# One copy and two squarings change places in ScalarE's order, in a graph attention kernel

## The chip, the cores and the metric

The kernel runs on one core of one Trainium2 chip. The metric is the device time of one execution in microseconds (us), as the median of several runs. In a profile, PE is TensorE (matmuls), PEld its weight loads, DVE is VectorE, ACT is ScalarE, POOL is GpSimd and SP is SyncE, which here issues nearly all the DMAs. L586 is line 586 of the kernel. PSUM is the memory that matmuls write; the kernel hands it out in pieces of 128 x 512 (banks, as its code calls them) and in pairs of two such pieces.

## The reference, cut to what matters

Sixteen images x[b] of 1024 nodes with 256 channels pass through two layers that share one 1024 x 1024 matrix adj. Everything is float32.

```python
# layer 0
fea  = x.transpose(0, 2, 1)                       # 256 x 1024 of an image
c    = mean(fea, axis=1)                          # one mean per node
A    = abs(abs(sigmoid(c_n - c_m) - 0.5) - 0.5) * 2
g    = relu((fea @ (adj * A)) * para)             # the "query graph": queries by channel
k, v = split(x @ kv_w)                            # 4 heads of 64
x1   = layernorm(x + softmax(q k^T * scale) v)    # over the channels
# layer 1
h    = relu(x1 @ w1_loop + adj @ (x1 @ w1_neigh) + b1)
h    = relu(h  @ w2_loop + adj @ (h  @ w2_neigh) + b2)
out  = layernorm(x1 + (x1 + h) * 0.5)
```

Two places matter here. One is the product of fea with the weighted matrix (the queries). The other is the layernorm of the attention's sum: it subtracts the mean, squares what is left, sums the squares over the channels and scales.

## The kernel before, in words

The program is one long list of instructions written out by hand, image by image (`run()`, L972 on); no scheduler moves anything. Each engine takes its own instructions in the order in which the Python code issues them, and a semaphore wait holds back an instruction whose data or buffer isn't ready.

For image b the loop first runs four attention units (`Attention`: scores, exponentials, denominators, outputs). Between the units it does the second layer of earlier images and prepares the weighted matrix of image b + 1. After the units, for 14 of the images, come these steps, which stand in the branch `elif more` (L1151 on):

- Steps 0 to 3 of the queries of image b + 1 (`FastQueries.step`, L560 to L577). The product is made by Strassen's method in the form with seven products, which are summed over four steps k. At each step seven matmuls run, each of 128 x 512, which the profile shows as two passes ("x2"). The sums stand in PSUM: products 1 and 6 in the two halves (banks) of one buffer, 2 and 7 in a second, 5 and 3 in a third, and 4 in a bank of its own. In step 3 the order is 1, 6, 2, 7, 4, 5, 3. The right factors come from VectorE (`times_adj`, `right`, `pair`, L494 to L496 and L542 to L558); product 6 takes the one that L551 makes.
- Beside step 1 the last attention results of image b are added up (`att.add`). Beside step 2, after its first four products, `norm.mean()` (L306 to L311) lets VectorE make the mean and subtract it from the two tiles of x, and `norm.squares()` (L313 to L316) lets ScalarE square the two tiles.
- `q.load_para()` and `kv.load()` issue three DMA loads on SP's queue.
- `FastQueries.end` (L579 to L596) puts the seven products together into the queries qT. ScalarE copies product 1 from PSUM to a tile P1 (L586); VectorE then makes the additions L587 to L590, the sums of the squares (`norm.sum_squares`, handed in as `between`, L318 to L322: two reductions L321 and one small addition), and the additions L592 to L594.
- `kv.run` (L409 on) makes keys and values of image b + 1 by the same method, first the key product 1 (L402), whose PSUM buffer is the one in which products 1 and 6 stood before. Three such buffers exist (`bufs=3`), and two single banks.
- In the middle of `kv.run`, `norm.variance` makes the reciprocal deviation (a small matmul L252, L326 on VectorE, a power on GpSimd, L328) and `q.scale` multiplies the queries by para (L600, L601).

Tiles of 128 x 1024 in SBUF (the squares, P1, U, para, kv_sums, adj and many others) come from one pool of 25 buffers (`row_tile`) that are handed out in the order of the code. A new owner waits until the last reader of the old one is done.

Of the kernel before, what the change touches and what calls it, by code (L numbers as in the profile page):

```python
# [18 lines left out]
def kernel(  # L19
# [79 lines left out]
    def row_tile(name):  # L99
        return work.tile([P, N], F32, tag="row", name=name, bufs=ROWS)  # L100
# [85 lines left out]
    def store(n, rows):  # L186
        for h in range(2):
            nc.sync.dma_start(out=far_adj[n][h], in_=rows[h])
# [275 lines left out]
    class Queries:  # L464
# [42 lines left out]
        def end(self):  # L507
            qT = work.tile([P, NC, N], F32, tag="qT", name=f"qT_{self.b}")
            for cb in range(NC):
                nc.vector.tensor_mul(qT[:, cb, :], self.pg[cb], self.para[cb])  # L510
                nc.scalar.activation(qT[:, cb, :], qT[:, cb, :], AF.Relu, scale=QSCALE)
            return qT

    class FastQueries(Queries):
# [61 lines left out]
                x_n, w_n = terms[n]  # L576
                nc.tensor.matmul(self.p[n], x_n[:, k, :], w_n, start=(k == 0), stop=(k == TJ - 1))  # L577

        def end(self, between):  # L579
            qT = work.tile([P, NC, N], F32, tag="qT", name=f"qT_{self.b}")  # L580
            u = row_tile(f"U_{self.b}")
            h0, h1 = ts(0, FB), ts(1, FB)
            p = self.p
            add = nc.vector.tensor_add
            p1 = row_tile(f"P1_{self.b}")[:, h0]
            nc.scalar.copy(p1, p[1])  # L586
            add(u[:, h0], p1, p[6])  # L587
            add(qT[:, 0, h0], p1, p[2])
            add(u[:, h1], u[:, h0], p[7])
            add(qT[:, 1, h0], u[:, h1], p[4])  # L590
            between()
            add(qT[:, 1, h1], u[:, h1], p[5])  # L592
            add(u[:, h0], u[:, h0], p[5])
            add(qT[:, 0, h1], u[:, h0], p[3])  # L594
            self.qT = qT
            return qT  # L596
# [375 lines left out]
    def run():  # L972
# [11 lines left out]
        q = Queries(0, x_first)  # L984
# [41 lines left out]
        qT = q.end()  # L1026
# [3 lines left out]
        for b in range(B):  # L1030
            more = b + 1 < B
            att = Attention(b, xB, qT, kT, v)
            c1, c2, c3 = (convs.get(b - k) for k in (1, 2, 3))
            both = Joined(c1, c2) if c2 else None
            if c1 and more:
                xb, blocked = coming
            if c2 and more:
                c2.load_h1()

            def load_next():  # L1040
                nonlocal coming
                if b + 2 < B:
                    coming = load_x(b + 2, str(b + 2)), load_blocked(b + 2, str(b + 2))

            def gap0():
                row = means(q, xb, str(b + 1))
                c1.inner()
                if both:
                    c2.load_x()
                    both.fetch(2, 3)  # L1050
                    both.left(nc.gpsimd)
                row()
                ready["xT"] = channel_major(blocked, f"xT_{b + 1}")

            def weigh_first():
                q.times_adj(0)
                q.times_adj(TJ)
                q.right(0)

            def gap1():  # L1060
                for t in (0, TJ):
                    q.load(t)
                if both:
                    both.fetch(1, 4)
                    both.run({1: (lambda: q.left(nc.gpsimd),),
                              2: (lambda: att.add(0, 1),),
                              6: (lambda: q.likeness(0), lambda: c3 and c3.moments()),
                              7: (lambda: q.likeness(TJ),),
                              5: (weigh_first,),
                              4: (lambda: c3 and c3.finish(out[b - 3]),),  # L1070
                              3: (c1.turn_blocks,)})
                else:
                    q.left(nc.gpsimd)
                    for t in (0, TJ):
                        q.likeness(t)
                    store("01", rows01)
                    c1.first(rows01, lambda: (att.add(1), adj_sums(rows01, 1), adj_sums(rows01, 2), weigh_first()))
                    c1.turn_blocks()

            def gap2():  # L1080
                if both:
                    c2.last()

            between = [gap0, gap1, gap2] if c1 and more else []
            if more:
                q = (FastQueries if c1 else Queries)(b + 1, xb)
            for u in range(len(UNITS)):
                att.scores(u)
                if u == 1 and between:
                    kv = KeysValues(b + 1, ready["xT"])  # L1090
                    kv.sums()
                if u == 3 and between:
                    for t in (2, TJ + 2, 3, TJ + 3):
                        q.load(t)
                    for t in (2, TJ + 2, 3, TJ + 3):
                        q.likeness(t)
                    q.right(1)
                if u and (not between or u != 2 and not both):
                    att.add(u - 1)
                att.outputs(u)  # L1100
                if u == 2 and more:
                    if c1:
                        for t in (1, TJ + 1):
                            q.load(t)
                            q.likeness(t)
                            q.times_adj(t)
                    else:
                        for t in range(3):
                            q.load(t)
                            q.weigh(t)  # L1110
                if u < 3 and between:
                    between[u]()
                if u == 0 and more and not between:
                    means(q, xb, str(b + 1))()
            norm = BlockedNorm(xB, att.sums, str(b))
            if more and not c1:
                kv = KeysValues(b + 1, ready["xT"])
                for t in range(3, NT):
                    q.load(t)
                for t in range(3, NT):  # L1120
                    q.likeness(t)
                tiles[2] = adj_blocked(2)
                q.times_adj(3)
                q.step(0)
                q.times_adj(4)
                q.step(1)
                att.add(3)
                for mt in (3, 5, 6, 7):
                    tiles[mt] = adj_blocked(mt)
                q.load_para()  # L1130
                q.times_adj(5)
                q.step(2)
                q.step(3)
                norm.mean()
                q.times_adj(6)
                q.times_adj(7)
                q.step(4)
                norm.squares()
                norm.sum_squares()
                q.step(5)  # L1140
                q.step(6)
                kv.sums()
                kv.load()
                norm.variance()
                xB = load_blocked(b + 1, f"a{b + 1}")
                q.step(7)
                qT = q.end()
                load_next()
                kT, v = kv.run(later=lambda: (norm.scale(), norm.spread(), turn_adj((2, 3))))
                turn_adj((5, 6, 7))  # L1150
            elif more:  # L1151
                q.pair(2)
                q.step(0)
                q.step(1, lambda: att.add(*((2, 3) if both else (3,))))
                q.pair(3)
                q.step(2, lambda: (norm.mean(), norm.squares()))
                q.load_para()
                kv.load()
                q.step(3)
                qT = q.end(norm.sum_squares)  # L1160
                xB = load_blocked(b + 1, f"a{b + 1}")
                load_next()
                kT, v = kv.run(norm.variance, q.scale)
                if not c2:
                    adj_sums(rows01, 3)
                norm.scale()
                norm.spread()
            else:
                c2.load_h1()
                c2.load_x()  # L1170
                both.fetch(2, 3)
                c1.inner()
                both.left(nc.gpsimd)
                both.fetch(1, 4)
                both.run({1: (lambda: att.add(3),), 2: (norm.mean, norm.squares, norm.sum_squares), 7: (norm.variance,),
                          5: (norm.scale, norm.spread)})
                c1.turn(0)
                c2.last()
                c1.turn(1)
            convs[b] = GraphConv(b, norm.x1T, norm.nodes)  # L1180
# [16 lines left out]
    with tc.manual_schedule():  # L1197
        run()
# [14 lines left out]
    with tc.If(count < P):  # L1213
        with tc.For_i(0, B, 1) as b:
            xb = load_x(b, "z")
            xT = channel_major(load_blocked(b, "z"), "xT_z")
            q = Queries("z", xb)
# [48 lines left out]
```

## Time and profile before

| quantity | value |
|---|---|
| median of 3 runs | 2163.99 us (2163.22 to 2164.79) |
| the profiled execution | 2163.48 us |
| its span, first to last instruction | 2161.6 us |
| granted TensorE clock, mean | 0.999 of full speed |
| time of one image in the middle of the run (first key product to first key product) | 133.1 us |
| squares L316 | 32 times, 1.06 us each |
| copy P1 L586 | 14 times, 0.57 us each |
| additions L587 | 14 times, 0.69 us each |
| para and kv_sums loads, issue to landing | 3.9 us and 5.7 us (medians) |
| bytes moved by DMA | 290.73 MB, 134 GB/s over the span |

The profile is of one execution. Its page gives each engine's busy time over the whole span. The list of waits sums up, for each pair "who waited for whom", the idle time of the waiting engine, with the number of waits and the longest one. The timeline lists instructions of an engine by start time; neighbours of one kind are merged into one row with their number ("x2"), and square brackets give the idle time of the engine before the row and what ended it. The ends of matmuls are modelled, so the distance between two starts says more about TensorE than a duration does. Instructions of the same kind repeat almost to the hundredth of a microsecond from image to image, so that one image can stand for the others.

### The profile page before, as it was taken

The numbers are of one execution on the slowest core, as the hardware profiler recorded it, in microseconds if no ns is written. First come the engines' busy times: TensorE is split into PE (matmuls) and PEld (weight loads), VectorE is DVE, ScalarE is ACT, GpSimd is POOL, SyncE is SP. The second block draws the span as 40 slices with busy tenths as digits, with TensorE's granted clock in tenths as the row PEclk, the third lists the DMA queues.
The fourth block names the chain that finished last, engine by engine and source line by source line (L and its number), as shares of the span: only waits on it lengthen the run. The fifth ranks groups of instructions, "written<-read, shape, count | busy, mean of one in ns | idle before, by whom it ended". The sixth has DMA issues, their size and how long they took to land.

```text
span 2161.6 us, 23756 instructions
## 1 busy us (share of the span) xinstructions
PE 2146.5 (99%) x8360; PEld 1021.1 (47%) x8360; DVE 1904.5 (88%) x2350; ACT 1041.0 (48%) x1374; POOL 362.7 (17%) x201
## 2 busy tenths in 40 slices
PE   9999999999999999999999999999999999999998
PEld 5344444444444444454544445454454444544354
DVE  5999988988999899899898998989889898998965
ACT  5745535545345454445443554445553445535412
POOL 1010120211303113030120302203021130211021
PEclk9999999999999999999999999999999999999999
DMA  9393654736558265472755627555374563733442
GB/s 236 117 146 117 148 154 110 164 97 134 148 128 182 86 132 156 130 173 88 122 167 127 160 88 120 172 127 156 88 134 159 127 156 106 140 134 90 125 137 99
DMA packets 612191, 290.73 MB, mean 134 GB/s; under 512 B 504800, under 2 KB 569696, under 8 KB 612064
## 3 DMA queue, kind: packets, MB, share of 16 engines
q1 hardware_dynamic: 611792, 288.87, 54.5%
q8 instruction: 68, 1.11, 0.2%
q14 instruction: 59, 0.48, 0.1%
q10 hardware_dynamic: 272, 0.26, 0.0%
HBM read 242.35 MB, written 46.72 MB: 134 GB/s over the span
## 4 chain that ended last, share of the span: by engine, by line


## 5 line engine op out<-in xcount | busy, mean ns | idle before, releaser
L628 ACT ACTIVATE pr<-s 128x1024 f32<-128x1024 f32 x512 | 476.1, 1054 | 175.0 <-PE s L625 174.2
L634 DVE TENSOR_TENSOR acc<-acc,pr 128x1024 f32<-128x1024 f32 x384 | 487.2, 1269 | 40.8 <-DVE acc L634 0.5
L625 PE MATMUL s<-qT,kT 64*128 64x512 f32 x2048 | 456.8, 596 | 0.0
L647 PE MATMUL av<-pr,v 128*64 128x512 f32 x2048 | 453.6, 595 | 0.0
L625 PEld LDWEIGHTS s<-qT,kT 64*128 64x128 f32 x2048 | 191.6, 186 | 236.6 <-ACT pr L628 112.5
L328 POOL TENSOR_TENSOR rstd<-rstd,neg_half 128x32 f32<-128x32 f32 x16 | 99.8, 6238 | 1125.6 <-DVE rstd L326 1125.6
L647 PEld LDWEIGHTS av<-pr,v 128*64 128x64 f32 x2048 | 141.3, 137 | 298.7 <-issue 291.6
L490 ACT ACTIVATE wg<-c_row,c_col 128x1024 f32<-128x1024 f32 x128 | 146.1, 1141 | 75.5 <-DVE accB L636 66.1
L496 DVE SCALAR_TENSOR_TENSOR wg<-wg,adj 128x1024 f32<-128x1024 f32 x128 | 150.0, 1210 | 12.3 <-ACT wg L491 12.3
L931 PE MATMUL hu_ps<-adj,R 128*128 128x512 f32 x360 | 158.0, 595 | 0.0
L491 ACT ACTIVATE wg<-wg 128x1024 f32<-128x1024 f32 x128 | 135.3, 1057 | 4.1
L316 ACT ACTIVATE sq<-xB_a 128x1024 f32<-128x1024 f32 x32 | 33.7, 1056 | 211.5 <-DVE xB_a L311 210.4
L577 PE MATMUL g_ps<-wg,S 128*128 128x512 f32 x224 | 116.4, 601 | 0.0
L577 PE MATMUL g_ps<-T,S 128*128 128x512 f32 x224 | 115.7, 598 | 0.1
L632 DVE TENSOR_TENSOR acc<-pr,pr 128x1024 f32<-128x1024 f32 x64 | 83.2, 1300 | 31.6 <-ACT pr L628 31.6
L577 PE MATMUL g_ps<-wg,x 128*128 128x512 f32 x224 | 109.0, 599 | 0.0
L931 PE MATMUL hu_ps<-adjT,t 128*128 128x512 f32 x240 | 105.7, 592 | 0.0
L931 PEld LDWEIGHTS hu_ps<-adj,R 128*128 128x128 f32 x360 | 67.3, 190 | 78.9 <-issue 78.9
L636 DVE STREAM_TRANSPOSE accB<-acc 128x1024 f32<-128x1024 f32 x64 | 79.7, 1246 | 2.2
L947 ACT COPY snap<-hu_ps 128x512 f32<-128x512 f32 x15 | 8.8, 585 | 150.3 <-PE hu_ps L931 150.3
L639 DVE TENSOR_REDUCE den_part<-accB 128x32 f32<-128x1024 f32 x64 | 78.1, 1220 | 2.2
L819 PE MATMUL h_ps<-w2n_sb,uT 128*128 128x256 f32 x240 | 72.7, 385 | 0.0
(204 smaller groups left out, 2997.2 us busy)
## 6 DMA issues: line engine op xcount, KB each, us to landing
adj<-in_adj_dram SPq DMA_DIRECT2D x128, 512.0 KB, 5.1
adj<-adjT SPq DMA_DIRECT2D x120, 512.0 KB, 10.2
para<-in_L_gnn_para_dram SPq DMA_DIRECT2D x32, 512.0 KB, 3.9
xB_a<-in_x_dram SPq DMA_DIRECT2D x128, 128.0 KB, 4.3
x1d<-xB_a SPq DMA_DIRECT2D x128, 128.0 KB, 3.5
x<-x1d SPq DMA_DIRECT2D x16, 1024.0 KB, 15.1
xB<-in_x_dram SPq DMA_DIRECT2D x120, 128.0 KB, 4.5
x<-in_x_dram SPq DMA_DIRECT2D x15, 1024.0 KB, 7.0
```

Source lines behind the costliest of these rows:

```text
L328: nc.gpsimd.tensor_tensor(self.rstd, self.rstd, neg_half, ALU.pow)
L490: nc.scalar.activation(wg, self.c_row, AF.Abs, bias=self.c_col[:, t:t + 1], scale=-1.0)
L491: nc.scalar.activation(wg, wg, AF.Tanh, scale=-0.5)
L496: nc.vector.scalar_tensor_tensor(wg, wg, 1.0, self.adj.pop(t), op0=ALU.add, op1=ALU.mult)
L577: nc.tensor.matmul(self.p[n], x_n[:, k, :], w_n, start=(k == 0), stop=(k == TJ - 1))
L625: nc.tensor.matmul(ps[:, ts(s, FB)], self.kT[rows, pair, ts(mt, P)], self.qT[rows, pair, ts(j, FB)], start=True, stop=True)
L628: nc.scalar.activation(pr, ps, AF.Exp)
L632: nc.vector.tensor_add(acc, self.pr[0], pr)
L634: nc.vector.tensor_add(acc, acc, pr)
L636: nc.vector.transpose(accB, acc)
L647: nc.tensor.matmul(pav[s * HD:(s + 1) * HD, :], self.v[:, mt, pair * P + s * HD:pair * P + (s + 1) * HD], self.pr[mt][:, ts(s, FB)], start ...
L931: nc.tensor.matmul(dst, self.x[n][:, k, :], half_adj[w][:, k, :] if w else of_rows(rows, k), start=(start and k == 0), stop=(k == TJ - 1), ...
```

## The change

The squaring of the two tiles of x is no longer issued beside step 2 but inside `FastQueries.end`, right after ScalarE's copy of product 1. In ScalarE's order the copy L586 then stands ahead of the two squares L316, in each of the 14 images that go through `FastQueries`. The row buffers of the squares are taken from the pool at that later place too, after those of para, kv_sums, U and P1. The numbers of lines below L586 move by one.

```diff
-        def end(self, between):
+        def end(self, between, aside):
             qT = work.tile([P, NC, N], F32, tag="qT", name=f"qT_{self.b}")
...
             p1 = row_tile(f"P1_{self.b}")[:, h0]
             nc.scalar.copy(p1, p[1])
+            aside()
             add(u[:, h0], p1, p[6])
...
-                q.step(2, lambda: (norm.mean(), norm.squares()))
+                q.step(2, norm.mean)
                 q.load_para()
                 kv.load()
                 q.step(3)
-                qT = q.end(norm.sum_squares)
+                qT = q.end(norm.sum_squares, norm.squares)
```

## The prediction

> **What bounds the kernel now.** I read the page's busy times first, then the list of waits, then the timeline around one hand-over between the query graph and the keys, engine by engine.
>
> ```profile
> PE 2146.5 (99%) x8360; PEld 1021.1 (47%) x8360; DVE 1904.5 (88%) x2350; ACT 1041.0 (48%) x1374; POOL 362.7 (17%) x201
> ```
>
> TensorE works nearly all the time, so only an edit that lets its matmuls start earlier can shorten the span; time saved on ScalarE (48%) or VectorE (88%) counts only where TensorE waits for it. The waits show one such chain:
>
> ```profile
> ACT sq L316 <- DVE xB_a L311: 210.4, 16, 16.2
> DVE U L587 <- ACT P L586: 23.2, 14, 1.7
> PEld k_ps L402 <- DVE U L587: 15.4, 14, 1.2
> ```
>
> Each of the 14 images whose queries go through `FastQueries` has it once: ScalarE's squares (L316) wait for the subtraction of the mean (L311), the copy P1 (L586) stands behind them, VectorE's first addition (L587) waits 1.7 us for P1, and the first key product (L402) waits for that addition, since it writes the PSUM buffer that P1 and the addition read. The idle time given is not yet what TensorE loses. For that I take its start times:
>
> ```profile
> 1043.52 1.02 PE L577 MATMUL g_ps<-wg,x 128*128 128x512 f32 x2
> 1044.53 1.13 PE L577 MATMUL g_ps<-T,S 128*128 128x512 f32 x2
> 1045.49 1.02 PE L577 MATMUL g_ps<-wg,x 128*128 128x512 f32 x2
> 1046.35 1.02 PE L577 MATMUL g_ps<-wg,S 128*128 128x512 f32 x2
> 1047.21 1.02 PE L577 MATMUL g_ps<-T,x 128*128 128x512 f32 x2
> 1048.06 1.02 PE L577 MATMUL g_ps<-T,S 128*128 128x512 f32 x2
> 1048.92 1.02 PE L577 MATMUL g_ps<-wg,S 128*128 128x512 f32 x2
> 1050.21 1.13 PE L402 MATMUL k_ps<-xT,kvw_sb 128*128 128x512 f32 x2 [0.27 <-DVE U L587]
> 1051.17 1.05 PE L406 MATMUL v_ps<-kvw_sb,xT 128*128 128x128 f32 x8
> 1052.07 1.02 PE L402 MATMUL k_ps<-xT,kvw_sb 128*128 128x512 f32 x2
> 1052.93 1.05 PE L406 MATMUL v_ps<-kvw_sb,xT 128*128 128x128 f32 x8
> ```
>
> The seven rows with g_ps are step 3, products 1, 6, 2, 7, 4, 5, 3 in that order, each in two passes. Product follows product every 0.86 us; the first key product comes 1.29 us after product 3, so it is 0.43 us late. It also takes 0.96 us until its successor starts, while the second key product takes 0.86: the second pass of a product that had to wait comes 0.10 us late too. ScalarE and VectorE in the same stretch:
>
> ```profile
> 1046.77 2.19 ACT L316 ACTIVATE sq<-xB_a 128x1024 f32<-128x1024 f32 x2 [13.63 <-DVE xB_a L311]
> 1048.87 0.57 ACT L586 COPY P<-g_ps 128x512 f32<-128x512 f32 x1
> ```
>
> ```profile
> 1045.45 2.36 DVE L311 TENSOR_TENSOR xB_a<-xB_a,mean 128x1024 f32<-128x1024 f32 x2
> 1049.47 0.69 DVE L587 TENSOR_TENSOR U<-P,g_ps 128x512 f32<-128x512 f32 x1 [1.66 <-ACT P L586]
> ```
>
> ScalarE is idle for 13.63 us and then does the copy last.
>
> **What the Trainium skill says.** "TensorE: Matmul & The Clock Gate", section "Architectural detail: the array is 16× 32×32, not 1× 128×128", has ScalarE and VectorE as strict FIFOs, while TensorE may pull a weight load ahead of matmuls in flight. The trace agrees: P1 could not pass the squares although its data were there 3 us before, and a product that waited shows its two weight loads together and a late second pass. "Perfetto Trace Analysis", section "Tensor Engine Instruction (MATMUL, LD_WEIGHTS)", says that a matmul's end is an estimate; it shows here as 1.02 us given for products that follow each other every 0.86, and is why I count starts and not the idle 0.27. "PSUM — Partial Sum Buffer", section "PSUM bank collisions raise a hardware error ⚠️", lets engines work on different banks at once; P1 reads the bank of product 1 while products 2 and 7 go to others, so an earlier copy needs no pause of TensorE. No run shown tests that.
>
> **The change part by part.** No instruction is added or removed; two squares (2 x 1.06 us) go behind one copy (0.57 us) on ScalarE.
>
> *P1.* It waits for the tile that products 1 and 6 share, so for product 6, whose estimated end is 1044.53 + 1.13 = 1045.66. ScalarE is idle then; I put the copy at 1045.7 to 1046.3, 3.1 us earlier.
>
> *The squares.* They wait for L311, whose first half lets them start at 1046.77. P1 is over 0.5 us before, so they cost nothing more; the cover is this 0.5 us. If product 6 came later than that, the squares would move by the difference. They end at 1048.9 as now, and their only readers, the two reductions L321, start in VectorE's queue at 1052.06 now and about 1050.3 then (next item), still 1.4 us behind them.
>
> *VectorE.* L587 no longer waits for ScalarE but for L311 ahead of it, over at 1047.8. The additions L587 to L590 then run from 1047.75 to about 1050.3, and what they need (product 7 ends at 1047.37, product 4 at 1048.23) is there. L321 and L592 to L594 follow, 1.7 us earlier than now, up to L436 at about 1056.0. There L326 needs the small matmul of the variance, which follows TensorE: that matmul is at 1057.40 now and 0.54 earlier then, so VectorE will idle some 1.2 us before L326. The stall goes from L587 to L326, where nothing of TensorE waits.
>
> *TensorE.* L587 will be over at about 1048.4; the first key product is due at 1048.92 + 0.86 = 1049.78. So there is 1.3 us of slack and the wait ends. Gain per image: 0.43 (late start) + 0.10 (late second pass) = 0.54 by the unrounded starts. What is late next? The second key product takes the buffer of products 2 and 7, free after L589 (about 1049.6, due 1051.5); the second value product takes product 4's bank, free after L590 (about 1050.3, due 1052.4). The waits of about 0.05 us inside the key and value products come from copies that TensorE itself releases, and stay.
>
> *SP and buffers.* The squares' two row buffers are now taken after those of para, kv_sums, U and P1, so these rotate. By the waits in the two programs' instruction order, the para loads now wait for the end of step 0 (about 1030.4) and the kv_sums load for product 3 of step 1 (1033.8); the loads are issued at 1033.82 to 1036.24 now, so none gets later. They move into a stretch (1028 to 1034 us) in which the windows view has the DMA engines at 0.01, out of one at 0.77. The next load in SP's queue, xB_a at 1037.48, keeps its wait, product 4 of step 1. The squares wait for an adj load issued at about 1014 to 1021. No wait on TensorE changes, and the buffers' next owners, the exponentials of the first attention unit, start over 10 us after their last readers. Cost: nothing.
>
> *Sum.* The timeline gives the late start 14 times: 0.37 in the first of these images, 0.43 in twelve, 0.52 in one, together 6.1 us; 0.105 x 14 = 1.5 us for the second passes. Together 7.6 us. The profiled execution took 2163.48 (span 2161.6 and 1.9 around it), so 2155.9 (span 2154.0); the median of before is 0.5 higher, so 2156.4. Two costs are not shown. The change-over from graph to keys without a wait: it costs nothing where key and value products alternate in this stretch (0.86 to 0.90 us apart, with waits that were met), and 0.09 us where TensorE goes from attention products to other shapes; I take nothing, and keep 0.09 x 14 = 1.3 us as the upper end. And that the late second pass stays: 1.5 us. A gain beyond 7.6 could come only from the 0.26 us that step 3 loses at product 6 (1.01 in place of 0.86, then 0.10), which waits for VectorE's T (L551) and isn't touched; I allow 0.5 us. Own range: 2155.4 to 2158.5.
>
> **The rivals.**
> *Half of it comes back inside the keys.* VectorE serves key and value buffers in a fixed order, and a matmul there may now be the one that waits. For it: TensorE already loses 0.05 here and there. Against: all these releases move by 1.7 us, the matmuls by 0.54. It would give about 3.8 us, half: 2160.2, within what counts as no change.
> *VectorE sets the period.* It is 88% busy and step 3 waits for it (L551). If its queue were full from one image to the next, the 0.54 us would reappear at product 6: 2164, no change. Against: in each image it idles before L667 for TensorE's den_ps (14.2 us over 14 waits) and at the start of attention units, so TensorE sets its time.
> *Slower.* P1 now blocks the squares. If product 6 ends late, the squares, the reductions L321, the variance and behind it TensorE's key products follow. Place: product 6 of step 3, which waits for VectorE. It decides from about 3 us: 0.5 until the squares move, 1.4 until L321 does, and 1.2 of idle time before L326. Each further us costs TensorE 1 us per image; 1 us in 14 images, with the gain lost, is 2178. Against: that product waits 0.15 us now, and 13 of the 14 images show the same within 0.1.
> That the order doesn't change is excluded: P1 stands ahead of both squares in the built program in all 14 images.
>
> **How the numbers follow.** What a measurement here can tell from no change is 0.2%, 4.3 us. Forecast 2156.4: 0.84. Half comes back (2160.2): 0.05. VectorE sets the period (2164): 0.06. Slower (2178): 0.05. Faster is the first alone, 0.84; same 0.05 + 0.06 = 0.11; slower 0.05. Range: from 2155.2 to 2160.3, its own range and the half case, 0.89 less what own bounds may miss.
>
> **What would show it.** Right: U no longer waits for P in the list of waits, nor k_ps for U; P1 about 1 us ahead of the squares' start; the first key product 0.86 us after product 3; VectorE idle before L326 by about 1.2 us; an image's period shorter by 0.54 us. Wrong: the wait of step 3 on T grows by 0.5 us (VectorE's period), a new wait of k_ps or v_ps on VectorE (half), or squares that start after 1046.8 on this clock (slower).

## The result and the profile after

The changed kernel takes 2157.04 us (median of 9 runs, 2156.72 to 2158.55), the kernel before in the same runs 2163.61: a ratio of 0.997 (95% interval 0.996 to 0.9981), 6.6 us or 0.30% faster. The forecast was 2156.4. The profiled execution took 2157.04 us, its span is 2155.3 (6.3 less than before).

The list of waits of the changed kernel, with the busy line of its page ahead of it; each wait gives total us, times, longest:

```profile
PE 2142.7 (99%) x8360; PEld 1021.6 (47%) x8360; DVE 1903.6 (88%) x2350; ACT 1042.7 (48%) x1374; POOL 358.2 (17%) x201
```

```profile
ACT P L586 <- PE g_ps L577: 178.2, 14, 15.1
ACT sq L316 <- DVE xB_a L311: 23.1, 16, 11.5
DVE rstd L326 <- PE sum_ps L252: 18.5, 16, 1.2
PEld g_ps L577 <- DVE T L551: 14.1, 26, 0.8
```

The waits of U for P and of k_ps for U are gone. ScalarE's long wait is now P1's, for its product. VectorE's stall has moved to L326, and step 3's wait for T is what it was in the list of before:

```profile
PEld g_ps L577 <- DVE T L551: 13.9, 25, 0.9
```

The same hand-over as in the prediction, one image, TensorE's timeline of the changed kernel (start, us):

```profile
1040.34 1.02 PE L577 MATMUL g_ps<-wg,x 128*128 128x512 f32 x2
1041.36 1.13 PE L577 MATMUL g_ps<-T,S 128*128 128x512 f32 x2
1042.32 1.02 PE L577 MATMUL g_ps<-wg,x 128*128 128x512 f32 x2
...
1045.75 1.02 PE L577 MATMUL g_ps<-wg,S 128*128 128x512 f32 x2
1046.61 1.02 PE L402 MATMUL k_ps<-xT,kvw_sb 128*128 128x512 f32 x2
1047.47 1.05 PE L406 MATMUL v_ps<-kvw_sb,xT 128*128 128x128 f32 x8
```

The first key product comes 0.86 us after product 3 (1.29 before) and takes 0.86 until its successor starts (0.96 before). ScalarE and VectorE of the changed kernel, whose addition U is now L588:

```profile
1042.52 0.58 ACT L586 COPY P<-g_ps 128x512 f32<-128x512 f32 x1 [12.56 <-PE g_ps L577]
1043.54 2.19 ACT L316 ACTIVATE sq<-xB_a 128x1024 f32<-128x1024 f32 x2 [0.44 <-DVE xB_a L311]
```

```profile
1042.29 2.36 DVE L311 TENSOR_TENSOR xB_a<-xB_a,mean 128x1024 f32<-128x1024 f32 x2
1044.57 0.68 DVE L588 TENSOR_TENSOR U<-P,g_ps 128x512 f32<-128x512 f32 x1
...
1047.15 2.34 DVE L321 TENSOR_REDUCE sq_part<-sq 128x32 f32<-128x1024 f32 x2
...
1054.04 0.19 DVE L326 TENSOR_SCALAR rstd<-sum_ps 128x32 f32<-128x32 f32 x1 [1.22 <-PE sum_ps L252]
```

P1 sits in ScalarE's idle time, the squares still start with L311's first half, and U follows L311 without a gap.

**Where 1.3 us went.** The last matmul of the program, in the timeline of before and then of the changed kernel:

```profile
2151.63 0.19 PE L1209 MATMUL good_ps<-ones_sb,good 128*1 128x1 f32 x2
```

```profile
2143.98 0.19 PE L1210 MATMUL good_ps<-ones_sb,good 128*1 128x1 f32 x2
```

It starts 7.65 us earlier, the forecast sum. But from its end to the end of the span before took 2161.6 - 2151.8 = 9.8 us and the changed kernel 2155.3 - 2144.2 = 11.1. VectorE and SP do the same there at the same distances until SP takes the branch that ends the list of ordinary work (`tc.If(count < P)`). Behind it SP makes eight waits (EVENT_SEMAPHORE), among them the one for the landing of the last stores. The view of that line, of before and then of the changed kernel, gives for SP the first and last start of these waits, and the start of the branch:

```profile
L1213 SPq EVENT_SEMAPHORE  x8: 17/17/17, 2157.9 to 2160.2; - x8
L1213 SPq COMPARE_BRANCH  x1: 50/50/50, 2157.4 to 2157.4; - x1
```

```profile
L1214 SPq EVENT_SEMAPHORE  x8: 17/17/17, 2153.3 to 2153.9; - x8
L1214 SPq COMPARE_BRANCH  x1: 50/50/50, 2149.8 to 2149.8; - x1
```

SP's first instruction behind the branch comes 0.5 us after it before, and 3.6 us after it now. In the changed kernel's trace the last store has landed at 2152.2, 1.1 us before SP's first instruction behind the branch: there SP, and not the store, sets the end. The changed kernel does no other work there, but the trace has 1356 instructions of SP ahead of the branch instead of 1380: as many DMA issues (885), and 24 fewer separate wait instructions, since the rotated buffers need fewer.

### The profile page after: what moved, and what is told of

It reads as the page before. It is cut to its first block, busy times and chain, and to the rows that moved or that the text cites. A ratio compares the mean times of both kernels' runs of the same rounds, so it can differ in the third digit from the quotient of the medians.

```text
span 2155.3 us, 23725 instructions
## 1 busy us (share of the span) xinstructions
PE 2142.7 (99%) x8360; PEld 1021.6 (47%) x8360; DVE 1903.6 (88%) x2350; ACT 1042.7 (48%) x1374; POOL 358.2 (17%) x201
## 4 chain that ended last, share of the span: by engine, by line
## 5 line engine op out<-in xcount | busy, mean ns | idle before, releaser
L586 ACT COPY P<-g_ps 128x512 f32<-128x512 f32 x14 | 8.2, 585 | 178.2 <-PE g_ps L577 178.2
```

## The experiments

Three questions were open: whether the gain comes from the order or from the buffers that rotate with it, how much room P1 has, and what lengthened the end. A fourth was whether TensorE sets the period, so that the next wait in step 3 can be taken too. Every edit is shown against the changed kernel. Times in brackets are those of before in the same runs.

**Order alone.**

```diff
+        def take(self):
+            self.sq = [row_tile(f"sq_{self.name}_{cc}") for cc in range(NC)]
+            for cc in range(NC):
+                nc.gpsimd.memset(self.sq[cc][:, 0:1], 0.0)
...
-                q.step(2, norm.mean)
+                q.step(2, lambda: (norm.mean(), norm.take()))
```

> ScalarE's order as in the changed kernel (P1 ahead of the squares), but the squares' two row buffers are taken where they were taken before the change (two one-column writes by the idle GpSimd take them beside step 2), so para, kv_sums, U and P1 have their old buffers. Theory 'order': TensorE's wait at the first key product is gone, its last matmul ends 7.6 us earlier than before; U waits for nothing on ScalarE. If the changed kernel's 1.3 us longer end (11.1 in place of 9.8 us from the last matmul to the end) comes with SP's instruction list, which has 24 fewer instructions in the changed kernel and is back to the old length here within one, the end is 9.8 again and the time about 2156.0; if the longer end comes from the order, 2157.0. Rival 'buffers' (the gain comes from the earlier para and kv_sums loads and the rotated buffers): 2163.6, as before the change.

Measured: 2156.23 (2164.01), ratio 0.9964 (0.9951 to 0.9978). TensorE's product 3, its first key product and its last matmul:

```profile
1045.64 1.02 PE L583 MATMUL g_ps<-wg,S 128*128 128x512 f32 x2
1046.50 1.02 PE L408 MATMUL k_ps<-xT,kvw_sb 128*128 128x512 f32 x2
...
2143.87 0.19 PE L1216 MATMUL good_ps<-ones_sb,good 128*1 128x1 f32 x2
```

The key product comes 0.86 us after product 3, and the last matmul ends at 2144.06, 7.76 us earlier than before. SP has 1381 instructions ahead of the branch here, and the branch is followed as quickly as before (first and last starts again):

```profile
L1220 SPq EVENT_SEMAPHORE  x8: 17/17/17, 2150.1 to 2153.0; - x8
L1220 SPq COMPARE_BRANCH  x1: 50/50/50, 2149.7 to 2149.7; - x1
```

The end takes 10.3 us, not the 9.8 that were expected: the last store lands 8.8 us after the last matmul here, 8.3 before. The order carries the whole gain.

**Buffers alone.**

```diff
-            nc.scalar.copy(p1, p[1])
             aside()
+            nc.scalar.copy(p1, p[1])
```

> The squares are issued inside end() as in the changed kernel, but ahead of P1: ScalarE's order is that of before, the buffers are taken late as in the changed kernel, and para and kv_sums are loaded early. Theory 'order': TensorE loses 0.43 + 0.10 us at the first key product of each of the 14 images again; with the longer end of the changed kernel 2164.9, without it 2163.6. Rival 'buffers': 2157.0.

Measured: 2164.03 (2164.01), ratio 0.9999 (0.9991 to 1.0008). ScalarE and then TensorE in its timeline:

```profile
1046.44 2.13 ACT L316 ACTIVATE sq<-xB_a 128x1024 f32<-128x1024 f32 x2 [13.64 <-DVE xB_a L311]
1048.48 0.57 ACT L587 COPY P<-g_ps 128x512 f32<-128x512 f32 x1
```

```profile
1048.59 1.02 PE L577 MATMUL g_ps<-wg,S 128*128 128x512 f32 x2
1049.83 1.13 PE L402 MATMUL k_ps<-xT,kvw_sb 128*128 128x512 f32 x2 [0.21 <-DVE U L588]
```

The stall is back, 0.38 us in place of 0.43, since the two squares take 2.13 us together here and 2.19 before; the cause of that is open. The last matmul ends 0.9 us earlier than before, but the branch is followed late (3.7 us) and the end takes 11.3. These two cancel in the time. SP issues the para loads of this image at 1029.19 here and at 1033.82 before, and nothing comes of it.

**One square ahead.**

```diff
-            nc.scalar.copy(p1, p[1])
-            aside()
+            aside(0)
+            nc.scalar.copy(p1, p[1])
+            aside(1)
```

> One square ahead of P1, the other behind it; otherwise the changed kernel. Theory 'slack': the square starts when L311's first half is done, P1 ends about 1.7 us later, U starts about 0.6 us later than in the changed kernel and ends about 0.7 us before the first key product is due: the whole gain stays, 2157.0 (0.86 us from product 3 to the key product), although VectorE waits about 0.6 us for P1 again. Rival 'each part of P1's delay counts': half of the gain, about 2160.4.

Measured: 2157.34 (2164.01), ratio 0.9971 (0.9959 to 0.9983). VectorE's U and TensorE around it:

```profile
1045.49 0.69 DVE L593 TENSOR_TENSOR U<-P,g_ps 128x512 f32<-128x512 f32 x1 [0.52 <-ACT P L591]
```

```profile
1046.08 1.02 PE L581 MATMUL g_ps<-wg,S 128*128 128x512 f32 x2
1046.94 1.02 PE L406 MATMUL k_ps<-xT,kvw_sb 128*128 128x512 f32 x2
```

VectorE waits for P1 in every image, and the key product still comes 0.86 us after product 3. The last matmul ends 7.3 us earlier than before (7.65 in the changed kernel): half of the move brings all but 0.3 us of the gain.

**Four and seven further copies ahead of P1.**

```diff
-            p1 = row_tile(f"P1_{self.b}")[:, h0]
+            p1_row = row_tile(f"P1_{self.b}")
+            p1 = p1_row[:, h0]
+            for _ in range(4):
+                nc.scalar.copy(p1_row[:, h1], p[1])
             nc.scalar.copy(p1, p[1])
```

The second of these two runs has `range(7)` in the same place.

> The changed kernel with four further copies of product 1 ahead of P1 on ScalarE (into the unused half of P1's row). Theory 'slack': P1 ends 1.9 to 2.3 us later than in the changed kernel, U is over 0.5 to 0.9 us before the first key product is due, the squares start about 1 to 1.5 us later and end before VectorE comes to L321: 2157.0, nothing lost. Rival 'each part of P1's delay counts': about 1.9 x 14 = 27 us more.

> As the one before with seven further copies: P1 ends 3.3 to 4.0 us later than in the changed kernel, U is over 0.55 to 1.25 us after the first key product is due. Theory 'slack': (0.55 to 1.25) + 0.10 us lost in each of 14 images, 9 to 19 us more than the changed kernel: 2166 to 2176, and the list of waits has k_ps behind U again. If the slack were larger than worked out: 2157.0.

Measured: 2156.51 with four (2163.88), ratio 0.9965 (0.9952 to 0.9978), and 2178.56 with seven, ratio 1.0067 (1.0051 to 1.0082). With four, VectorE's U:

```profile
1045.88 0.69 DVE L591 TENSOR_TENSOR U<-P,g_ps 128x512 f32<-128x512 f32 x1 [0.84 <-ACT P L589]
```

With seven, ScalarE, VectorE's U and then TensorE:

```profile
1052.25 4.29 ACT L588 COPY P<-g_ps 128x512 f32<-128x512 f32 x7 [12.55 <-PE g_ps L577]
1056.44 0.59 ACT L589 COPY P<-g_ps 128x512 f32<-128x512 f32 x1
1056.92 2.02 ACT L316 ACTIVATE sq<-xB_a 128x1024 f32<-128x1024 f32 x2
```

```profile
1057.06 0.69 DVE L591 TENSOR_TENSOR U<-P,g_ps 128x512 f32<-128x512 f32 x1 [2.69 <-ACT P L589]
```

```profile
1055.48 1.02 PE L577 MATMUL g_ps<-wg,S 128*128 128x512 f32 x2
1057.81 1.12 PE L402 MATMUL k_ps<-xT,kvw_sb 128*128 128x512 f32 x2 [1.30 <-DVE U L591]
1058.77 1.05 PE L406 MATMUL v_ps<-kvw_sb,xT 128*128 128x128 f32 x8
```

VectorE's wait of 0.84 us makes no key product late (the last matmul ends 0.4 us later than in the changed kernel, over the whole run); one of 2.69 us makes the key product late by 2.33 - 0.86 = 1.47 us and its second pass by 0.10, so 1.57 x 14 = 22 us, and the last matmul ends 22.3 us later than in the changed kernel. The expectation's 9 to 19 us was too low because the seven copies put P1 off by 4.2 us (1052.25 to 1056.44), 0.60 us each from start to start, and not 0.47 to 0.57. The room is 2.69 - 1.47 = 1.2 us; the working of the prediction had 1.3.

**SP's list made as long as before.** The 24 added loads of 4 bytes stand in the middle of the program, and nothing reads them.

```diff
                     both.fetch(1, 4)
+                    if b == 8:
+                        pad = const.tile([1, 24], F32, name="pad")
+                        for i in range(24):
+                            nc.sync.dma_start(out=pad[:, i:i + 1], in_=b1[i:i + 1].rearrange("(p o) -> p o", o=1))
```

> The changed kernel with 24 loads of 4 bytes each issued by SP once, in image 8, ahead of a store for which SP waits many us anyway; SP's instruction list has the length of before again. Theory 'fetch' (SP's first instruction behind the branch at the end comes late or soon by where the list ends): the gap from SP's branch to its next instruction is 0.5 us in place of 3.6, the end from the last matmul on is 9.8 to 10.3 us in place of 11.1, and the time 2156.0 to 2156.3; the last matmul ends as in the changed kernel. Rival (the longer end comes from the landing of the last stores): 2157.0.

Measured: 2156.40 (2163.88), ratio 0.9965 (0.9951 to 0.9978). The last matmul ends at 2144.26, the end takes 10.5 us:

```profile
L1218 SPq EVENT_SEMAPHORE  x8: 17/17/17, 2150.3 to 2153.4; - x8
L1218 SPq COMPARE_BRANCH  x1: 50/50/50, 2149.8 to 2149.8; - x1
```

The gap behind the branch is 0.5 us again, as expected; the end is 0.6 us shorter than the changed kernel's, less than expected. SP's last waits here run to 2153.4 (2153.9 in the changed kernel), because they then wait for the landing of the last stores, which lies between 7.8 and 9.1 us after the last matmul in the ten traces, one of each kernel. So the end is set by the later of the two, the gap or the landing. The medians differ by 0.6 us (2156.40 against 2157.04, of different runs) and their ratios' intervals overlap: the gap is shown by the trace, its share of the time is not told apart by the times.

**Product 2 ahead of product 6 in step 3.**

```diff
-            for n in (1, 6, 2, 7, 4, 5, 3) if k == TJ - 1 else (1, 2, 3, 5, 7, 6, 4):
+            for n in (1, 2, 6, 7, 4, 5, 3) if k == TJ - 1 else (1, 2, 3, 5, 7, 6, 4):
```

> The changed kernel with step 3 in the order 1, 2, 6, 7, 4, 5, 3: product 6, which waits for VectorE's T, comes 0.86 us later. Theory 'TensorE sets the period': the 0.15 us that product 6 waits and the 0.10 us of its second pass go, 0.25 x 13 = 3.3 us less: about 2153.7; P1 starts about 0.8 us later and delays the squares by about 0.4 us, which nothing waits for. Rival 'VectorE sets the period': the wait moves to another product of step 3, 2157.0.

Measured: 2154.09 (2164.01), ratio 0.9954 (0.994 to 0.9967). TensorE in step 3, products 1 and 2 merged in the first row:

```profile
1038.71 1.88 PE L577 MATMUL g_ps<-wg,x 128*128 128x512 f32 x4
1040.42 1.02 PE L577 MATMUL g_ps<-T,S 128*128 128x512 f32 x2
1041.28 1.02 PE L577 MATMUL g_ps<-wg,S 128*128 128x512 f32 x2
```

Two products in 1.71 us and product 6 in 0.86: nothing waits. The last matmul ends 3.7 us earlier than in the changed kernel. VectorE, 88% busy, does not set the period: had it done so, the wait would have gone to another product, and the time would have stayed at 2157.

**Both.** The edit of the first experiment (order alone, with the old buffers) together with the one just above:

> Old buffers as in the first of these runs and product 2 ahead of product 6 in step 3: the last matmul ends about 3.7 us earlier than with the changed kernel, the end is about 10 us long: about 2152.6.

Measured: 2152.36 (2163.88), ratio 0.9947 (0.9934 to 0.9961): the fastest of all, 0.53% below before. Its last matmul ends at 2140.93, 3.2 us earlier than in the changed kernel and not the 3.7 expected, and the end takes 9.3 us and not 10. The time comes close to the expectation because these two misses cancel.

## Why the prediction was right

- *P1 and the squares.* P1 was put just behind product 6; it starts 0.03 us after that product's modelled end (1041.36 + 1.13). The squares follow 0.44 us after P1 and were not moved, close to the 0.5 us that was named as cover. The copy ran while TensorE wrote product 2, and the next product still started 0.86 us after it (1042.32, 1043.18).
- *VectorE.* U follows L311; L321 comes 1.4 us after the squares' end, as worked out; the stall before L326 is 1.22 us (forecast 1.2).
- *TensorE.* Both parts went, 0.43 us of late start and 0.10 of late second pass. An image takes 132.6 us from first key product to first key product, 0.5 less. The change-over without a wait costs nothing: 0.86 us like any other product. Its upper end of 1.3 us was not needed. One reading was not a good sign: two weight loads together stand in the trace of before at the second key product too (at 1051.96), which lost nothing. What the product that waited had to itself is that its first weight load started with its first pass (both at 1050.21), where in the changed kernel the load starts at 1046.18 and the pass at 1046.61.
- *SP and buffers.* Costed at nothing for the loads, rightly: the run with the buffers alone takes the time of before. What the step missed is that the rotation shortens SP's list, and that this comes back at the end.
- *The term that was off.* The sum took TensorE's 7.6 us to be the gain in time, which supposes that what follows the last matmul is the same. It was 1.3 us longer in the changed kernel's trace, so 7.65 became 6.3 in the span and 6.6 in the medians. That is inside the range given. That the time itself missed by only 0.6 us is in part luck: the gain was 1.0 us too high, and the median of before, 2163.99 when the forecast was made, is 2163.61 in these runs. The upper end of its own range, 2158.5, falls short of the two costs named beside it (2156.4 + 1.3 + 1.5 = 2159.2); the full range, up to 2160.3, has room for them, and nothing hangs on it here.
- *The rivals.* Half coming back inside the keys and VectorE setting the period fell with the changed kernel's trace and with product 2 first. A slower kernel came only in the run with seven further copies, where U waited 2.69 us for P1 with room for 1.2, and by another way than the one named: TensorE waited for U. The squares, which the rival had in mind, ended at 1058.94 there and were read from 1059.66 on. The rival's threshold of about 3 us for a late product 6 was not tried.

## What to carry to other kernels

Put the instruction whose data are ready first, and that another engine waits for, ahead of one that merely stands earlier in the code: on ScalarE, which took its work in the order of the code here, everything behind a waiting instruction waited with it. Work out the room first (here 1.2 us), since within it half of the move did as well as the whole, to 0.3 us. And sum such gains from the distance between starts on the bounding engine, with the second pass of a product that had to wait, not from the idle time in the list of waits (0.27 and 1.1 us here, where 0.54 was lost).

## What was not expected of the hardware

- SP's first instruction behind the branch at the end came 0.5 us after it with 1380 or 1381 instructions ahead (four kernels), and 2.7 to 3.8 us after it with 1356 (the other six). Lengthening the list by 24 brought 0.5 back. ScalarE shows the same at its own branch: 0.5 us with 1994 to 2067 instructions ahead (four kernels), 2.6 to 2.9 with 1956 to 1969 (six).
- The Trainium skill, "Runtime: NRT & Kernel Launch", section "Instruction fetch mechanics", offers a reason: instructions are streamed in blocks of 256, and a taken branch whose target lies outside the two blocks at hand waits for a fetch. The traces support it. They list the fetches of instructions as packets of DMA queue 14, and the view of the DMA from 3 us before SP's branch to the end has 7 of them in the changed kernel and 6 with SP's longer list. Over the ten kernels the number is 4, and one more for each of SP, ScalarE and GpSimd whose gap is the longer of its two (GpSimd's are 0.2 and 0.5 us). The packets do not name their engine, so that SP's 3 us are spent on this fetch is argued and not shown.
- The two kernels in which SP's longer gap is 2.7 us and not 3.5 to 3.8 (four and seven further copies) are those of the six in which ScalarE's is 0.5. Whether fetches of several engines hold each other up was not tested.
- A matmul that waited for its operands or its buffer lost a further 0.10 us at its second pass, in the two places read here (the key product and product 6: 0.96 us to the next start in place of 0.86), and lost it no more when it didn't wait. Why is open.
